# Other orders for the written work lists of a one-core convolution and attention kernel

## The chip, the cores and the metric

The kernel runs on one core of a Trainium2 chip. The metric is the device time of one execution in microseconds (us). The engines are TensorE (PE, matrix products), VectorE (DVE), ScalarE (ACT), GpSimd (POOL) and SyncE (SP, which issues most of the transfers between the chip's memory and the core's buffers). Each engine works through its own instructions in order; semaphores hold it back where it needs another engine's or a transfer's result.

## The reference

The input is 8 images of 512 channels by 32 x 32 points, all in 32-bit floats. Each image goes through two layers with a residual connection:

```python
# layer 0
x = x + L0(_gn(x))          # _gn: 32 groups of 16 channels
#   t = silu(bn(conv1x1(x)))              512 -> 512 channels, halves y0, y1
#   twice: z = silu(bn(conv3x3(y)))       256 -> 256
#          q, k, v = conv1x1(z)           4 heads of 64
#          a = softmax(q (k + rw + rh)^T / 8)
#          y_next = y + silu(bn(conv1x1(a v)))
#   silu(bn(conv1x1(concat(y0, y1, y2, y3))))     1024 -> 512
# layer 1
x = x + L1(_gn(x))
#   h = prune(relu(bn(depthwise3x3(x))), 4.0)
#   prune(relu(bn(conv1x1(h))), 0.001)            512 -> 512
```

`prune` sets a whole channel to zero when its largest magnitude lies under the limit. Attention runs over all 1024 points of an image, in each of the two inner blocks.

## The kernel before

The images come one after another (b = 0 to 7). A channel block of 128 partitions by 1024 points is the usual tile. The program does not write its instructions in a fixed sequence of loops. Each stage adds small closures, called pieces here, to named queues (`add`, line 306), and `go` (line 309) takes them from the queues in the order of a written list of names: `Q*3` is three pieces of queue Q. There are four lists: FIRST (lines 45 to 60) is all of image 0 up to the middle of its layer 1, HEAD the start of images 1 to 7 (with what remains of the image before), TAIL the rest of images 1 to 6, and LAST the rest of image 7. For image 7 HEAD leaves out the words that prepare a following image (`PREPARATION`).

`InOrder` (line 93) ties every instruction of PE, DVE, ACT and SP to the one issued before it on its engine, so that these four engines execute in exactly the order of the lists. Its line 103 makes all those calls; almost every row of the profile has line 103, and the rows must be told apart by their tiles. POOL is not tied.

The names that matter, with the function that defines them:

- `conv3` (line 737), the 3x3 convolution in a transformed form: `d` makes the input's combinations on DVE, `P` the products on PE (16 products of 128 x 128 x 128 and one 1 MB weight tile for each piece), `Rc` (ACT) and `R`, `B`, `E` (DVE) transform back, `Ez` (ACT) is the activation into z. `X` and `S` load ACT's tables for exp and silu.
- `qkv` (line 903): `k`, `v`, `q` on PE; `ka`, `va`, `qa` copy the results out. `kp` (image 0) adds the position terms on POOL; `kd` (later images) adds them by a transfer from POOL's queue that accumulates into kr, read from r in the chip's memory.
- `positions` (line 894): `rk` builds a tile `pos` on DVE and stores it to r, four times in all, in image 0.
- `attention` (line 984), 32 steps for each inner block: `s` scores on PE, `e` exponential on ACT into a work buffer, `p` adds up e on DVE, `w` values on PE, `h` (ACT) and `z` (DVE) join the two accumulators; `n` sums over partitions on PE, `nr` reciprocal on DVE, `ns` spreads it over all partitions by 8 transfers (rw<-r) on SP, `nc` checks (ACT), and `sc` multiplies z by rw on DVE, four pieces.
- `cv2m` (line 1096): `m` (PE), `ma` (ACT), `mr` (DVE), the block's closing 1x1 convolution and residual.
- The large 1x1 convolutions use a seven-product scheme over quarters of the weights: layer 0's first (`ct`, `c ck cu ca`, `y yk yu ya`), its last (`quartered`, line 1262: `r0` to `r3`, `Q`, `K`, `u0 u1`, `a0 a1`, `x0 x1`) and layer 1's (`ot`, `o ok ou oa`, `O Ok Ou Oa`). Image 0 uses plain weights (`last_conv`, line 1123: `Q K u A x`), image 7 for its last two.
- `combine_weights` and `combine_more` (lines 1192 and 1223), queue `cw`, in image 0 only: 12 pieces that load weights into ht (ht<-in_w), add and subtract quarters into tiles `scomb` and store quarters and sums to the chip's memory (q<-ht, q<-scomb, s<-ht, s<-scomb).
- `layer1_front` (line 578): statistics `i im id iv ip ib`, normalised copy `b`, centre tap `bm`, eight taps `t` for each channel block on DVE, `l` relu, `lr` and `lp` the prune test. `layer1_back` (line 623): products `o`, ends `oa`, prune test `fr`, and `f`, the residual and the store of the output.
- `dp` loads the next image to pt (4 x 512 KB), `dx` loads the same image to xt again for the residual, `dw` loads wm2, `g gm gd gv gp gb ga` normalise pt; `rg` (line 1376) is the range check of the softmax sums: `least` and then `decide`, a matmul pk on PE and the flag on DVE.

Large weights pass through a ring of 5 buffers of 8 KB for each partition (`ring_load`, line 412): when a tile's product is issued, the load of the tile five places on follows on SP. Temporary tiles (e, sum, rw, pos, scomb, mid, ...) share one pool, `work`, of 11 buffers of 4 KB for each partition; a new tile waits until all that read or wrote its buffer before, transfers included, is done. So the order of the lists also decides which tiles share a buffer, and which engine waits for which transfer.

Of the kernel before, what the change touches and what calls it, by code (L numbers as in the profile page):

```python
# [15 lines left out]
P = 128  # L16
B, C, F = 8, 512, 32
# [27 lines left out]
FIRST = """  # L45
    g*6 gm gd gv g gp g gb gm gd ga gv ga c gp fo gb c ta0 ga ta0 ga ta0 ti0 fo ta2 to0*2 c ti0*2
    ca ta2*2 c rl ca ta1*3 ti2 ti1 to1 d ti1 d y ya to1 ti1 y ya ti2 to2 d ti2 d to2 rl d*2 y ya
    y ya P*2 Rc R Rc d dw d*3 R d*2 P Rc P*3 Rc R B*2 R B Rc R E Ez B Rc R E Ez ta0 k*3 ka kp k X
    ka q*4 ta0*2 qa*2 v ti0 to0 ta1*2 to0 s e ti0*2 kp ta1 v va v*2 va ti1 s ti1*2 w s*2 e*2 w s
    e*2 p*3 w s*2 p ta2 e w*2 to1 e s*2 w p*2 s e p e w to1 e w ta2 s h p z e ta2 s e w*2 p s*2  # L50
    ti2 e*2 p w to2*2 s e s w*2 e p w*2 ti2*2 s*2 e*2 w p*2 s*2 w h e w s e w s e p s w s e*2 p*5
    n nr p z rh ns e p nc sc s e w*2 s*2 w*2 e*2 s w s*2 w h s z w sc e*4 w p*4 s w*2 e w p*2 w
    nc p n dp h z S nr nc*2 ns sc*2 Q m ma K mr m ma m*2 ma*2 mr*2 Q K mr d*7 P*2 Rc R d P Rc R
    Rc d*2 R d P Rc d R B*2 P Rc R E B P Rc Ez R B E Ez k cw rk X k*3 ka kp ka kp cw*3 v*2 va v*2
    va q rk q qa q cw s e cw q qa s e p w s*2 e p e p w cw s*2 dx w e p s e p e s e p*2 w*3 s e w
    g s e w h z s*2 e w s e w s g*2 s w p s*2 e*2 cw e cw w*2 e s p*2 w*2 s*2 cw w p*2 e p e*3 rk
    p cw*2 h p s z e s e w s e w rk p g p w*2 p w s n p nr s*2 e ns p*2 sc e w e nc s*2 g*3 e w s
    e*2 s e p w h s e nc w s e g p*3 w*3 p*2 w*3 sc w p h z*2 Q S n nr nc ns sc Q gm m ma mr sc
    m*3 ma*2 mr*2 ma mr Q u Q A x gd u Q A x gv i gp nc i*3 Q im id Q iv ip ib b gb A x bm i ga*4
    t i t*3 ct Q ct Q A x i*2  # L60
"""

HEAD = """
    c*4 ck cu ct*2 ca cu t im c cu*2 c*2 id iv cu y ca t cu*2 ca yk ca y*2 ip y t*2 d yu d ya y
    ib yu d*2 P d yu d*2 b P Rc R b bm d P d*2 y Rc R Rc b d R d B P Rc l B lr R B P Rc R E B P
    Rc R E Ez*2 yu bm*2 y lp yu ya yu*2 k t*19 v*2 va k*2 ya*2 ka k ka v*2 va X l kd q*2 qa lr lp
    t kd q s e t q qa s e p w s e s e p w*2 s*2 e*2 w s*2 w*2 s e*2 w s w e*2 s p*5 h e l w s*2 w
    e*2 lr t s w*2 p*2 e s e s e t w s w*2 z e s*2 e w e s w s*2 h e p e w s*2 p*5 z w e*3 s*2 e
    t w e p*2 s*2 e*2 w*2 l lr w p ot s p*2 e p*3 lp w h z n nr nc ns p*2 w lp w s*2 w e s w*2
    e*2 w*3 p sc p sc nc S p ot h z n nr o ok o ns O Ok ou oa ot*2 O sc m sc ma m ma Ou Oa m mr  # L70
    ma m ma O o mr*3 Ou ou d o d ou o O*2 d*2 P Ou ou Ou d*2 o ou d Rc ou nc R oa d*2 Ou oa P Rc
    d nc O P R d*2 P Rc P R B Oa Rc P R Ou Oa B*2 Rc B Rc R E R E Ez*2 o O k*4 ou oa Ou Oa ka*2
    fr*3 v*2 va q*2 v*2 dp qa g va g q X kd f g f kd s e q qa fr f*2 dx s e w s*2 e w e s*2 w s*2
    e*4 p*2 w s g*3 p*3 g s w*2 e s w*2 e*2 s*2 w g h s w e*2 w p*4 s*2 w s*2 w p*2 s*2 e p w e*6
    p w*2 h s*2 e*2 z p*4 w p*2 s e s z e w p*2 s n nr ns e w*4 nc s nc s e w p e w h s*2 w sc w
    e w s*2 e*3 w s p e p sc p*4 w*4 z n h z nr S ns
"""

TAIL = """
    r2 r0 Q*3 r0 sc*2 r0*2 m*2 r1 m ma gm m nc gd ma gv r1 ma r3 mr*2 K mr r2 r3 gp r2 ma mr r1  # L80
    gb ga r1 K ga ct r2 Q r3 Q*4 u1 u0 r3 Q u0*4 Q u0 Q a1 Q a0 x0 a0 ga x0 i a0 x0 i*3 im u0 a0
    id x1 ga ct Q iv ip Q u1 x0 ib b i u1 i bm t u1 t Q*2 u1 t*2 u1*2 a1 x1 a1*2 x1*2 i*2 nc
"""

LAST = """
    Q*2 nc sc m sc nc rg m*3 ma*3 mr ma mr*3 Q A Q x i*2 im id Q iv ip Q ib Q A x b bm i*2 t*2 im
    id Q iv t*2 ip t*2 ib t b bm t*2 Q A x i*2 t Q l lr lp t im id t Q A iv ip t Q ib b bm t*4 x
    t A x t i*2 l lr o*2 t im id o iv t lp ip t ib o*2 rg b bm t*4 l lr t lp t*5 l lr lp o*20 oa
    o oa o*6 fr f oa*2 fr f oa*2 fr f oa*2 fr f
"""  # L90


# [1801 lines left out]
```

## Time and profile before

| what | value |
|---|---|
| median of 4 runs | 2582.24 us (2581.66 to 2582.9) |
| profiled run, its own time | 2583.75 us |
| its span, first to last instruction | 2581.8 us |
| granted TensorE clock, mean | 0.995 |
| busy: PE, DVE, ACT, POOL | 2535.8, 2074.2, 1205.5, 126.4 us |
| bytes moved by DMA | 284.38 MB, mean 110 GB/s |
| output stores (out<-xt) | 32 of 512 KB, 7.2 us to land (median) |
| image loads xt<-in_x, pt<-in_x | 32 of 512 KB each, 6.9 and 11.6 us |
| ring loads wring<-u | 96 of 1 MB, 4.8 us |
| row spreads rw<-r | 256 of 64 KB, 2.0 us |

The profile is of one execution. A row of a timeline has its start (us from the start of the span), its length, the engine, the line, the operation, output<-input, how many instructions were merged, and in brackets the idle time of the engine before it with what ended it. A row of waits has who waited for whom, the total, how often, and the longest. A row of windows has the stretch, its length, then for PE, PEld (weight load), DVE, ACT and POOL the busy time and the count, then PE's granted clock (1.00 is full), the busy share of the DMA engines, and GB/s. Each fp32 matmul is two records. The profiled run is compared with itself; times of runs are compared with the median.

### The profile page before, as it was taken

The numbers are of one execution on the slowest core, as the hardware profiler recorded it, in microseconds if no ns is written. First come the engines' busy times: TensorE is split into PE (matmuls) and PEld (weight loads), VectorE is DVE, ScalarE is ACT, GpSimd is POOL, SyncE is SP. The second block draws the span as 40 slices with busy tenths as digits, with TensorE's granted clock in tenths as the row PEclk, the third lists the DMA queues.
The fourth block names the chain that finished last, engine by engine and source line by source line (L and its number), as shares of the span: only waits on it lengthen the run. The fifth ranks groups of instructions, "written<-read, shape, count | busy, mean of one in ns | idle before, by whom it ended". The sixth has DMA issues, their size and how long they took to land.

```text
span 2581.8 us, 38500 instructions
## 1 busy us (share of the span) xinstructions
PE 2535.8 (98%) x15518; PEld 1329.9 (52%) x15518; DVE 2074.2 (80%) x2992; ACT 1205.5 (47%) x1595; POOL 126.4 (5%) x100
## 2 busy tenths in 40 slices
PE   7998999999999999999999999999999999999997
PEld 4463464644646346463464634646455554656443
DVE  7877599866988779886798868988699876998647
ACT  3634347353472634635355353644436454373524
POOL 1000000000000000000000000000000000000000
PEclk9999999999999999999999999999999999999998
DMA  9357141341414324052240612407133160422400
GB/s 347 120 174 254 60 153 36 105 164 59 148 33 149 115 71 141 32 183 80 74 145 17 225 39 82 137 19 245 32 110 94 50 214 31 140 65 86 123 17 34
DMA packets 116393, 284.38 MB, mean 110 GB/s; under 512 B 10608, under 2 KB 76400, under 8 KB 101872
## 3 DMA queue, kind: packets, MB, share of 16 engines
q1 hardware_dynamic: 108624, 263.76, 29.5%
q0 software_dynamic: 4032, 14.68, 3.1%
q10 hardware_dynamic: 3552, 3.41, 0.4%
q8 instruction: 124, 2.03, 0.3%
q14 instruction: 61, 0.50, 0.1%
HBM read 226.24 MB, written 38.80 MB: 103 GB/s over the span
## 4 chain that ended last, share of the span: by engine, by line
PE 72%; DVE 20%; DMA 3%; ACT 2%; issue 2%; SPq 1%; ACTq 0%; POOL 0%; DVEq 0%
PE ps_s L103 15%; PE ps_av L103 14%; PE ps_qk L103 8%; PE ps_q L103 7%; PE ps_c L103 6%; PE ps_cv L103 6%; PE ps_cv2q L103 6%; PE ps_m L103 4%; PE ps_v L103 4%; DVE ht L103 3%; DVE mid L103 3%; DVE sum L103 2%; SPq L103 1%; DVE y L103 1%; DVE vtmp L103 1%
## 5 line engine op out<-in xcount | busy, mean ns | idle before, releaser
L103 ACT ACTIVATE e<-ps_s 128x1024 f32<-128x1024 f32 x512 | 504.2, 1022 | 237.1 <-PE ps_s L103 185.5
L103 PE MATMUL ps_s<-qy,kr 64*64 64x512 f32 x4096 | 518.6, 592 | 6.1 <-ACT e L103 6.0
L103 PE MATMUL ps_av<-e,vt 64*64 64x512 f32 x4096 | 518.8, 593 | 0.0
L103 DVE TENSOR_TENSOR sum<-sum,e 128x1024 f32<-128x1024 f32 x384 | 468.5, 1220 | 58.0 <-ACT e L103 30.7
L103 DVE SCALAR_TENSOR_TENSOR ht<-xn,v_sb,ht 128x961 f32<-128x961 f32 (+1 forms) x256 | 319.3, 1252 | 8.3 <-ACT ht L103 3.1
L103 PEld LDWEIGHTS ps_s<-qy,kr 64*64 64x64 f32 x4096 | 172.5, 132 | 278.0 <-issue 133.0
L103 PEld LDWEIGHTS ps_av<-e,vt 64*64 64x64 f32 x4096 | 185.1, 133 | 253.5 <-issue 226.8
L103 PE MATMUL ps_qk<-z,wring 128*128 128x512 f32 x512 | 232.8, 598 | 2.3 <-ACT z L103 1.9
L103 PE MATMUL ps_q<-pt,wring 128*128 128x512 f32 x392 | 176.8, 594 | 0.0
L103 DVE TENSOR_TENSOR sum<-e 128x1024 f32<-128x1024 f32 x64 | 78.1, 1221 | 106.3 <-ACT e L103 66.8
L103 ACT COPY c<-ps_c 128x256 f32<-128x256 f32 x96 | 35.8, 373 | 262.8 <-PE ps_c L103 259.6
L103 PEld LDWEIGHTS ps_qk<-z,wring 128*128 128x128 f32 x512 | 94.6, 190 | 120.0 <-issue 99.6
L103 PEld LDWEIGHTS ps_c<-vt,wring 128*128 128x128 f32 x1024 | 118.7, 194 | 11.7 <-issue 6.7
L103 PE MATMUL ps_c<-vt,wring 128*128 128x128 f32 x1024 | 119.6, 277 | 4.8 <-DMA wring<-u 4.8
L103 PEld LDWEIGHTS ps_c<-kr,wring 128*128 128x128 f32 x1024 | 117.9, 192 | 11.4 <-issue 8.3
L103 PE MATMUL ps_v<-wring,z 128*128 128x256 f32 x512 | 117.9, 381 | 0.9 <-DVE kr L103 0.3
L103 PE MATMUL ps_c<-kr,wring 128*128 128x128 f32 x1024 | 118.1, 275 | 0.1
L103 PE MATMUL ps_c<-qy,wring 128*128 128x128 f32 x1024 | 117.0, 275 | 0.0
L103 PEld LDWEIGHTS ps_c<-qy,wring 128*128 128x128 f32 x1024 | 115.6, 192 | 0.0
L103 PE MATMUL ps_m<-z,wm_sb 128*128 128x512 f32 x256 | 113.9, 594 | 0.0
L103 PEld LDWEIGHTS ps_q<-pt,wring 128*128 128x128 f32 x392 | 71.7, 190 | 81.0 <-issue 72.5
L103 ACT ACTIVATE m<-ps_m,bi,sc 128x512 f32<-128x512 f32 x64 | 49.8, 778 | 134.9 <-PE ps_m L103 133.8
(189 smaller groups left out, 3298.6 us busy)
## 6 DMA issues: line engine op xcount, KB each, us to landing
wring<-u SPq DMA_DIRECT2D x96, 1024.0 KB, 4.8
wring<-q SPq DMA_DIRECT2D x28, 896.0 KB, 4.8
pt<-in_x SPq DMA_DIRECT2D x32, 512.0 KB, 11.6
rw<-r SPq DMA_DIRECT2D x256, 64.0 KB, 2.0
xt<-in_x SPq DMA_DIRECT2D x32, 512.0 KB, 6.9
out<-xt SPq DMA_DIRECT2D x32, 512.0 KB, 7.2
kr<-r POOLq DMA_DIRECT2D x28, 512.0 KB, 6.0
wring<-in_wqkv SPq DMA_DIRECT2D x16, 768.0 KB, 4.3
```

The costliest lines, as they stand in the source:

```text
L103: made = method(*args, **kwargs)
```

## The change

Only the four strings are changed. Each list holds the same pieces as before, and each queue keeps its own order; what differs is the order among queues, and with it the order of instructions on PE, DVE, ACT and SP, the sharing of work buffers, and the waits. The first 70 pieces of FIRST are the same. In FIRST the stores of weight sums (`cw`) and positions (`rk`), `dx`, `dw` and ACT's `S` stand elsewhere; in HEAD `dp`, `dx`, `f`, the taps `t` and `sc`; TAIL starts with `sc` instead of `r2 r0 Q`; in LAST the second `rg` and the closing `o oa fr f`.

```diff
@@ -45,48 +45,49 @@
 FIRST = """
     g*6 gm gd gv g gp g gb gm gd ga gv ga c gp fo gb c ta0 ga ta0 ga ta0 ti0 fo ta2 to0*2 c ti0*2
     ca ta2*2 c rl ca ta1*3 ti2 ti1 to1 d ti1 d y ya to1 ti1 y ya ti2 to2 d ti2 d to2 rl d*2 y ya
-    y ya P*2 Rc R Rc d dw d*3 R d*2 P Rc P*3 Rc R B*2 R B Rc R E Ez B Rc R E Ez ta0 k*3 ka kp k X
-    ka q*4 ta0*2 qa*2 v ti0 to0 ta1*2 to0 s e ti0*2 kp ta1 v va v*2 va ti1 s ti1*2 w s*2 e*2 w s
-    e*2 p*3 w s*2 p ta2 e w*2 to1 e s*2 w p*2 s e p e w to1 e w ta2 s h p z e ta2 s e w*2 p s*2
-    ti2 e*2 p w to2*2 s e s w*2 e p w*2 ti2*2 s*2 e*2 w p*2 s*2 w h e w s e w s e p s w s e*2 p*5
-    n nr p z rh ns e p nc sc s e w*2 s*2 w*2 e*2 s w s*2 w h s z w sc e*4 w p*4 s w*2 e w p*2 w
-    nc p n dp h z S nr nc*2 ns sc*2 Q m ma K mr m ma m*2 ma*2 mr*2 Q K mr d*7 P*2 Rc R d P Rc R
-    Rc d*2 R d P Rc d R B*2 P Rc R E B P Rc Ez R B E Ez k cw rk X k*3 ka kp ka kp cw*3 v*2 va v*2
-    va q rk q qa q cw s e cw q qa s e p w s*2 e p e p w cw s*2 dx w e p s e p e s e p*2 w*3 s e w
-    g s e w h z s*2 e w s e w s g*2 s w p s*2 e*2 cw e cw w*2 e s p*2 w*2 s*2 cw w p*2 e p e*3 rk
-    p cw*2 h p s z e s e w s e w rk p g p w*2 p w s n p nr s*2 e ns p*2 sc e w e nc s*2 g*3 e w s
-    e*2 s e p w h s e nc w s e g p*3 w*3 p*2 w*3 sc w p h z*2 Q S n nr nc ns sc Q gm m ma mr sc
-    m*3 ma*2 mr*2 ma mr Q u Q A x gd u Q A x gv i gp nc i*3 Q im id Q iv ip ib b gb A x bm i ga*4
-    t i t*3 ct Q ct Q A x i*2
+    y ya d P Rc R P d*3 Rc R d*2 P Rc R B P Rc R B*3 P*2 Rc R E Ez Rc R E Ez k*3 ka k ka kp X ta0
+    q*2 qa ta0*2 ti0*2 kp v s e v va v*2 va ta1 ti0 ta1*2 to0*2 q*2 qa ti1 dw s w e p s e s e w s
+    ti1 s ti1 to1 e*2 p w p*3 w s e w ta2 w s e w to1 s e p*2 s e w h z p s e p ta2*2 s w*2 e s w
+    s e s e ti2*2 w*2 p to2 s w p*2 ti2 e to2 s e w e s e w h p*2 s e s w s*2 e w e s*2 p*4 w*2 n
+    e nr e p z s p e p e s rh nc w e w s ns sc w*2 e s*2 w h s w*2 s e*4 w z sc w p s w*2 e w h p
+    nc p*5 n nr z ns sc*2 dp nc*2 Q m*2 ma*2 m*2 K ma mr Q ma mr*3 d*4 S K P*2 d*3 Rc R d Rc R P
+    Rc d*2 R d cw d B*2 P Rc R P Rc R E Ez B P B k Rc R E Ez cw k*2 ka X dx g k ka kp cw*3 kp rk
+    q*2 qa rk v*2 va v*2 va q s e q qa s e p cw*2 w s e p s e w*2 s*2 e w s*2 e*3 p*5 w s*2 e w e
+    p w*2 h z s e s w*3 cw s*2 e*2 w p cw w cw p*2 s g s e*3 w s*2 w e p*2 s e*2 p g s e w h s e
+    rk s p z w e s e w s cw*2 p e p w*2 g rk p*2 s n nr e s e p*2 w s*2 p g e ns g w*3 p nc s e h
+    s w e*2 s*2 e*2 p sc nc S p*2 w*3 g*2 p w*4 sc p z h z Q n nr Q gm nc ns sc m ma m ma sc mr m
+    ma nc gd gv gp m mr ma mr*2 Q*3 gb Q u A u x i*2 A x i*2 im id Q A iv ip x ib b bm t ga t
+    ga*3 i*2 t Q*2 ct*2 A t x i*2
 """
 
 HEAD = """
-    c*4 ck cu ct*2 ca cu t im c cu*2 c*2 id iv cu y ca t cu*2 ca yk ca y*2 ip y t*2 d yu d ya y
-    ib yu d*2 P d yu d*2 b P Rc R b bm d P d*2 y Rc R Rc b d R d B P Rc l B lr R B P Rc R E B P
-    Rc R E Ez*2 yu bm*2 y lp yu ya yu*2 k t*19 v*2 va k*2 ya*2 ka k ka v*2 va X l kd q*2 qa lr lp
-    t kd q s e t q qa s e p w s e s e p w*2 s*2 e*2 w s*2 w*2 s e*2 w s w e*2 s p*5 h e l w s*2 w
-    e*2 lr t s w*2 p*2 e s e s e t w s w*2 z e s*2 e w e s w s*2 h e p e w s*2 p*5 z w e*3 s*2 e
-    t w e p*2 s*2 e*2 w*2 l lr w p ot s p*2 e p*3 lp w h z n nr nc ns p*2 w lp w s*2 w e s w*2
-    e*2 w*3 p sc p sc nc S p ot h z n nr o ok o ns O Ok ou oa ot*2 O sc m sc ma m ma Ou Oa m mr
-    ma m ma O o mr*3 Ou ou d o d ou o O*2 d*2 P Ou ou Ou d*2 o ou d Rc ou nc R oa d*2 Ou oa P Rc
-    d nc O P R d*2 P Rc P R B Oa Rc P R Ou Oa B*2 Rc B Rc R E R E Ez*2 o O k*4 ou oa Ou Oa ka*2
-    fr*3 v*2 va q*2 v*2 dp qa g va g q X kd f g f kd s e q qa fr f*2 dx s e w s*2 e w e s*2 w s*2
-    e*4 p*2 w s g*3 p*3 g s w*2 e s w*2 e*2 s*2 w g h s w e*2 w p*4 s*2 w s*2 w p*2 s*2 e p w e*6
-    p w*2 h s*2 e*2 z p*4 w p*2 s e s z e w p*2 s n nr ns e w*4 nc s nc s e w p e w h s*2 w sc w
-    e w s*2 e*3 w s p e p sc p*4 w*4 z n h z nr S ns
+    ct c*4 ck cu*2 ct ca c cu im c*2 t id y cu*2 ca iv t cu y*2 t ca cu t ca yk y ip l d y yu d
+    ib ya b d*3 yu d yu P Rc d P R Rc d*2 R P d Rc R d*2 P Rc R B*2 b*2 P*2 Rc R B lr E Rc R B bm
+    y E Ez*2 y lp yu bm yu ya t yu t yu t*2 bm k v*2 t*8 ya va k ka k*2 t*3 ka v*2 t va l lr q*2
+    qa ya t*3 X q kd*2 s e lp q qa s e w s e s e w*2 s e s e w s p*3 s p e*2 p*3 t*2 w s*2 e w*3
+    s*2 w e t l h s e*2 w s*2 p w p ot e*3 s*2 e p*2 z w p s p*2 e*2 s p e p t lr w*4 s*2 w h s*2
+    z lp e w s*2 e*5 w p w s t p e w*2 s*2 e*2 p*3 n nr p l w*2 h p z nc s p w e ns lr lp s e w*3
+    s*2 w e nc e w*3 h p*4 ot n nr nc z ns nc ot o*2 ok ou S oa sc*2 ot O Ok O sc m sc ma m ma O
+    m*2 o*2 Ou Oa mr Ou ma mr*2 ma mr d ou O d*2 o d*2 ou P Rc d*2 Ou R ou d o P d*2 O Ou Rc ou
+    oa ou oa Ou Oa P Rc O P dp R*2 d Rc d P R P Rc B*2 R E B Ez Rc R o O B E Ez Ou k Ou ou q Oa q
+    qa oa k v ka v*3 va*2 k*2 ka q Oa g fr*2 X kd s e q qa kd f*2 fr g*2 s w e p s*2 e p w s*2 e
+    p e*2 w s*2 w s p*2 e*2 p*2 s fr w s*2 w*2 f w g e*4 f h s*2 e w e p*3 s w e g s e p w s*2 w
+    s e*3 s e w g*2 w p*2 g w p z w h s e s p w e w s e p*2 s p*3 e p w s dx e s e n nr nc z p ns
+    sc w*2 s e p w s e p w*2 h s w s*2 e p w*3 s w z sc e*2 p*2 e w*2 p w h z S n nr ns nc
 """
 
 TAIL = """
-    r2 r0 Q*3 r0 sc*2 r0*2 m*2 r1 m ma gm m nc gd ma gv r1 ma r3 mr*2 K mr r2 r3 gp r2 ma mr r1
-    gb ga r1 K ga ct r2 Q r3 Q*4 u1 u0 r3 Q u0*4 Q u0 Q a1 Q a0 x0 a0 ga x0 i a0 x0 i*3 im u0 a0
-    id x1 ga ct Q iv ip Q u1 x0 ib b i u1 i bm t u1 t Q*2 u1 t*2 u1*2 a1 x1 a1*2 x1*2 i*2 nc
+    sc*2 nc r2 r0 r2 r0 Q*3 gm gd r0 m ma m mr gv m r1 r3 Q r0 m Q ma mr ma mr r2 r1 gp gb ma mr
+    r1*2 r3 r2 r3 ga*2 K*2 Q u0 Q ct a0 Q u0 Q u1 r3 Q u0*3 a0 a1 x0 u0 i*2 x0 a0 x0 i Q x1 Q i*2
+    u0 i a0 im Q x0 id iv ip ga*2 ct ib b bm nc u1 Q u1*2 t u1 t Q*2 t u1 a1 t u1 x1 a1 x1 a1 x1
+    i*2
 """
 
 LAST = """
-    Q*2 nc sc m sc nc rg m*3 ma*3 mr ma mr*3 Q A Q x i*2 im id Q iv ip Q ib Q A x b bm i*2 t*2 im
-    id Q iv t*2 ip t*2 ib t b bm t*2 Q A x i*2 t Q l lr lp t im id t Q A iv ip t Q ib b bm t*4 x
-    t A x t i*2 l lr o*2 t im id o iv t lp ip t ib o*2 rg b bm t*4 l lr t lp t*5 l lr lp o*20 oa
-    o oa o*6 fr f oa*2 fr f oa*2 fr f oa*2 fr f
+    Q*2 sc nc*2 rg sc m ma m*2 ma mr*2 m ma*2 mr*2 Q A x i*2 Q*2 im Q A id iv ip Q ib b x i*2 bm
+    t im t Q id iv t*2 ip t ib b bm t*4 Q A x i*2 t l lr Q lp t im id Q A t*2 iv ip t ib b t*2 bm
+    t x t Q A x t o i*2 o*2 t im id l lr t o*2 iv ip t ib lp b bm t*2 l t lr rg t*2 lp t*5 l lr
+    lp o*22 oa*2 fr f oa o*3 oa fr f o*2 oa*2 fr f oa*2 fr f
 """
 
 
```

## Prediction

> **What bounds the kernel now.** I read the page's busy times and chain first.
>
> ```profile
> PE 2535.8 (98%) x15518; PEld 1329.9 (52%) x15518; DVE 2074.2 (80%) x2992; ACT 1205.5 (47%) x1595; POOL 126.4 (5%) x100
> ...
> PE 72%; DVE 20%; DMA 3%; ACT 2%; issue 2%; SPq 1%; ACTq 0%; POOL 0%; DVEq 0%
> ```
>
> PE is busy for 98% of the span, and the change leaves it the same 15518 matmuls. So nothing can be won but the time in which PE stands still or runs at half clock; that "busy" holds half-clock time too. The waits of PE, longest first, say where it stands, and their windows say in which list:
>
> ```profile
> PE pm L103 <- DVE mv L103: 13.6, 5, 8.1
> PE ps_s L103 <- ACT e L103: 6.0, 4, 3.4
> PE ps_c L103 <- DMA wring<-u: 4.8, 1, 4.8
> PE ps_dn L103 <- DVE sum L103: 3.8, 6, 0.9
> ```
>
> The first (8.1 us) and third (4.8 us, at 58 us) lie in the start of FIRST, whose first 70 pieces stay; the third waits for a load that those pieces issue. The second is the place to look at: PE, ACT and SP's queue around 250 us, each from its timeline, and PE's granted clock in between.
>
> ```profile
> 248.75 1.33 PE L103 MATMUL ps_s<-qy,kr 64*64 64x512 f32 x8 [2.11 <-ACT e L103]
> ...
> 258.39 1.09 PE L103 MATMUL ps_s<-qy,kr 64*64 64x512 f32 x8 [3.42 <-ACT e L103]
> ```
> ```profile
> 247.67 1.94 ACT L103 ACTIVATE e<-ps_s 128x1024 f32<-128x1024 f32 x2 [4.98 <-DMA s<-scomb]
> ...
> 257.31 1.02 ACT L103 ACTIVATE e<-ps_s 128x1024 f32<-128x1024 f32 x1 [4.89 <-DMA r<-pos]
> ```
> ```profile
> 235.16 2.51 SPq L103 DMA_DIRECT2D xt<-in_x  x4
> 237.71 2.82 SPq L103 DMA_DIRECT2D s<-scomb  x4
> 241.34 0.55 SPq L103 DMA_DIRECT2D ht<-in_w  x1
> 251.22 1.53 SPq L103 DMA_DIRECT2D s<-ht  x3
> 252.87 0.63 SPq L103 DMA_DIRECT2D r<-pos  x1
> ```
> ```profile
> 244.00:249.80 5.80, 3.69 (x36) 1.02 (x32) 4.71 (x4) 1.94 (x2) 0.00 (x0) 0.97 1.01 356
> 249.80:252.90 3.10, 3.10 (x20) 1.07 (x16) 1.57 (x3) 1.61 (x2) 0.00 (x0) 0.50 0.32 91
> 252.90:259.70 6.80, 3.38 (x32) 0.97 (x28) 6.76 (x9) 1.50 (x2) 0.00 (x0) 1.00 1.03 357
> 259.70:263.10 3.40, 3.40 (x20) 1.05 (x16) 3.19 (x3) 1.47 (x2) 0.00 (x0) 0.50 0.18 72
> ```
>
> An exponential e twice waits for a work buffer that a store still reads. SP's queue is in order: the image load xt (4 x 512 KB) sits just ahead of the stores of scomb; the next weight load (ht) takes until 251.2 while the DMA engines are full (share 1.01, 356 GB/s), and the store of pos, queued behind stores that need that load, leaves only at 252.87. Each stall is followed by some 3.4 us at clock 0.50. The timeline of PE has 104 score and value matmuls from 243.46 to 264.18 us; 4 of them back to back take 0.43 us, so they need 11.2 of 20.7 us: 9.4 us are lost here (0.1 off for the last one's end).
>
> **The change part by part.** The sum is made against the profiled run, 2583.75 us (span 2581.8, 1.95 around it), which lies 1.5 us above the median of the four runs.
>
> *FIRST, weight sums, positions and dx.* dx now comes in layer 1's key stage, some 21 us of PE work ahead of the last weight load, and so out of the full stretch. From each store's piece to the piece that takes its buffer next, counted in listed PE pieces (0.86 us a score or value piece, 1.72 a key, value or query projection), the cover was 6.9 us twice for scomb and 0.9 us for the last pos. In the new lists it is 9.5, 8.6, 4.3, 1.7, 3.5 and 5.2 us, and only one of the three short ones is taken by an e: 4.3 and 1.7 us are a scomb and a pos on DVE, which has slack (64.54 us busy in 200 to 285 us). A store needs its issue (0.6 us) and 2.4 us to land at least, 5.2 in the median, 9.1 at most. So DVE waits 1.5 and 2 us, of which I count half to reach PE, and e (3.5 us cover) 1 to 2 us: 3 us stay, 9.4 - 3 = 6.4 us gained. Bounds: all of it gained, or a loss of 3 us (a store landing after 9.1 us, three times, each 4 us over its cover).
>
> *Clock.* An idle time of 1.60 us (layer 1's first key product, 195.1 us) left the clock at full, one of 2.11 us halved it for 3.4 us (1.7 us lost). My 3 us are pieces under 2 us, so no half clock is added; one wait of 3 us would add 1.7. [...]
>
> *FIRST, elsewhere.* Close Ez of the second half now stands ahead of Rc on ACT at layer 1's keys (1.60 us idle on ACT z): 0.7 us won, but a weight sum (2 x 0.6 us) comes in on DVE there: nothing. dw (one load) moves past ring loads whose tiles are used five tiles later: nothing; without that cover 4.8 us, wring's landing.
>
> *HEAD, seven times.* The image period is 313.0 us, 308 of it PE's pieces at their back-to-back pace; most of the rest are switches that stay. What goes is in the waits of ps_dn: the softmax sums' second n waits for the last p on DVE, because sc0 and sc1 stand before it and wait for eight row spreads by DMA:
>
> ```profile
> 770.18 0.69 DVE L103 TENSOR_TENSOR z<-z,rw 128x512 f32<-128x512 f32 x1 [1.34 <-DMA rw<-r]
> ...
> 772.75 0.69 DVE L103 TENSOR_TENSOR z<-z,rw 128x512 f32<-128x512 f32 x1 [0.74 <-DMA rw<-r]
> ```
>
> In the new layer 0, sc0 and sc1 follow the last p, n and ns. DVE gets 2.1 us of waits and 1.3 us of work off the way to n; n1 begins 0.45 to 1.45 us (mean 0.97) behind the pieces' pace, 0.2 of it the switch. Gain 0.75 an image. What is late next: sc2, behind the second n's spreads, reaches the first m some 0.35 us late by the rows' durations. Net 0.4, bounds +1 and -1 (the longest n1 wait, either sign). The taps t no longer come 19 in a row after the first k: DVE is full there (40.45 of 40.80 and 29.43 of 30 us), but its work up to layer 0's last E is the same within 0.1 us (43.6 against 43.5 us), so the wait of 0.34 us at v stays. dp (pt load) moves ahead of the last two P of layer 1, past their ring loads and the accumulating kd loads of POOL; ring tiles have five tiles of cover, kd some 3 us: nothing, without cover 2 to 6 us (kd lands in 6.0). Output stores and dx come later, dx still some 20 us ahead of x: nothing. 7 x 0.4 = 2.8 us gained (-7 to +7).
>
> *TAIL.* sc comes first, so DVE waits about 5 us (eight spreads at 0.6 us of issue, 2.0 to land) without r's before it. The first product that needs all r0 has 17 us of PE pieces before it (Q, Q, half Q, three m, half Q, m), DVE's work to there 5 us of wait and 9 us of instructions: nothing; 3 us of cover. If it is gone, some 2 us an image.
>
> *LAST.* Its end is DVE's taps: flag waited for PE (1.25 us), on the way to the last tap.
>
> ```profile
> 2546.70 0.15 DVE L103 TENSOR_SCALAR flag<-pk 1x1 int32<-1x1 f32 x1 [1.25 <-PE pk L103]
> ...
> 2565.12 1.13 PE L103 MATMUL ps_pw<-ht,wring 128*128 128x512 f32 x2 [0.87 <-ACT pw L103]
> ```
>
> rg's second half now stands after the third lr, where PE comes to its matmul pk straight from the last statistics (iv), with no o pieces before it, and has it done long before DVE asks: 1.2 us gained. In the second row a product waited for an oa that reads the other half of its PSUM tile; in the new list no product stands behind an oa of its own tile: 0.8. Output stores keep their order: together 2 us (0 to 3).
>
> Sum: 2583.75 - 6.4 - 2.8 - 2.0 = 2572.5, less 1.5 to the median: **2571 us**.
>
> **The rivals.**
> - *The stall in FIRST stays in another place* (the 1.7 and 3.5 us covers): for it, DMA was full there and the sums keep their bytes; against it, the bytes of xt are gone from that stretch. Gain 2.8 + 2.0 only: 2577.4.
> - *Slower: layer 1's first P waits in every image.* In HEAD before, six pieces of 1.72 us lie between the last m and the first P of layer 1 (10.3 us); in the new list four (6.9 us). On the way stand ma (0.78), the last mr (0.6), four d (two at 1.2, the last two together 2.4) and ou (0.6): 6.8 us, so the cover is about nothing, and what delays DVE there, as sc2's wait, goes to PE. Against it: DVE is 51.26 of 60 us busy from 720 to 780, so it should come to m on time. It decides from (6.4 + 2.8 + 2.0)/7 = 1.6 us an image; at 3 us, 2571 + 21 = 2592 (one image's DVE wait for rw, longest 4.1, makes this the likely top).
> - *No difference:* PE's work is equal, and gains of FIRST are given back by half a microsecond to 1.5 an image: 2577 to 2587.
>
> **How the numbers follow.** The forecast 0.45 (2562 to 2575), FIRST's stall stays 0.17 (2575 to 2579), slower by P 0.28 (2587.5 to 2600), no difference 0.10. The measurement can tell about 0.2%, 5.2 us: faster is below 2577, slower above 2587.4. Half of the rival at 2577.4 is same. Faster 0.45 + 0.09 + 0.01 = 0.55, same 0.16, slower 0.29. The range leaves out 0.05 below 2558 (all of FIRST, +7 in HEAD) and 0.12 above 2595.
>
> **What would show it.** In the changed kernel's trace: no e row with a wait of over 2.5 us for DMA s or r, and clock 1.00 from 240 to 270 us (FIRST); the row ps_dn waiting for sum under 1 us in all and an image period of 312.6 us (HEAD); no row of PE waiting for kr at layer 1's first P (rival); flag without its 1.25 us (LAST). I am wrong if the image period grows: seven times any small wait outweighs the one stall.

## The result

The changed kernel takes 2579.35 us (median of 32 runs, 2575.61 to 2583.71); the kernel before, run beside it, 2582.69 us (median of 52 runs). The ratio is 0.9986, with a 95% interval of 0.9981 to 0.9991: 3.6 us (2.3 to 4.9) less, under the 0.2% that counts as a change here. 11 us had been forecast. The profiled run has a span of 2578.4 us, 3.4 less than before.

The busy times and the chain on the changed kernel's page, to be held against the two lines shown of the kernel before:

```profile
PE 2530.1 (98%) x15518; PEld 1309.9 (51%) x15518; DVE 2074.5 (80%) x2992; ACT 1206.9 (47%) x1595; POOL 143.5 (6%) x100
...
PE 91%; DVE 6%; DMA 1%; ACT 1%; SPq 1%; issue 0%; POOL 0%; ACTq 0%; DVEq 0%; POOLq 0%
```

The chain now runs through PE for 91% instead of 72%. That alone tells little: it says that DVE stands less often on the path, and not that PE loses less time. What PE waits for tells more:

```profile
PE pm L104 <- DVE mv L104: 12.2, 4, 8.0
PE ps_cv L104 <- DVE c L104: 5.1, 6, 0.9
PE ps_av L104 <- ACT e L104: 4.2, 1, 4.2
PE pv L104 <- DVE d L104: 3.9, 4, 1.4
PE ps_c L104 <- DMA wring<-u: 3.9, 1, 3.9
PE ps_pw L104 <- DVE wring L104: 2.2, 1, 2.2
PE ps_qk L104 <- ACT z L104: 2.0, 1, 2.0
...
PE ps_dn L104 <- DVE sum L104: 0.3, 1, 0.3
```

The waits of ps_s for e (four, 6.0 us) and of ps_dn for sum (3.8 us, now 0.3) have gone or shrunk, as forecast. Others are new or longer: ps_cv for c, six times 0.85 us, once in each TAIL; pv for d, two more than before, in TAIL of images 2 and 6; ps_av for e, 4.2 us in FIRST; ps_pw for wring in LAST. The wait of ps_qk for z stands elsewhere: 2.0 us at layer 0's keys in FIRST, instead of 1.6 at layer 1's.

Where the time went, list by list. A list's time runs from the start of its first product to that of the next list's; the records of PE were put to the pieces of the lists in order.

| stretch | before, us | changed, us | difference | forecast |
|---|---|---|---|---|
| up to the first product | 8.14 | 7.99 | -0.2 | 0 |
| FIRST | 327.95 | 323.53 | -4.4 | -6.4 |
| HEAD, seven | 1798.6 | 1788.9 | -9.7 | -2.8 |
| TAIL, six | 335.6 | 344.5 | +8.9 | 0 |
| LAST to its last product | 101.1 | 102.3 | +1.2 | -2.0 |
| last product to the end of the span | 10.4 | 11.2 | +0.8 | |
| sum | 2581.8 | 2578.4 | -3.4 | -11.2 |

HEAD wins more than three times what was forecast and TAIL gives nearly all of it back. Every sign that the forecast had named came true: no e of layer 1's attention in FIRST waits for a store, the clock is 1.00 from 240 to 270 us, ps_dn waits 0.3 us in all, no first P of layer 1 waits in images 1 to 7, flag waits no more, and the image period is 312.6 us in four images of six. That period was met by luck, because HEAD's extra gain and TAIL's loss cancel; with images 2 and 6 the mean is 313.0 us, against 312.9 before. The signs looked only where the forecast expected something.

**TAIL.** PE and DVE in TAIL of image 2 of the changed kernel, from their timelines:

```profile
912.97 0.39 PE L104 MATMUL pv<-d,g_sb 128*128 128x4 f32 x2 [0.72 <-DVE d L104]
...
921.88 1.88 PE L104 MATMUL ps_cv<-qy,wring 128*128 128x512 f32 x4
924.61 0.70 PE L104 MATMUL ps_cv<-qy,wring 128*128 128x512 f32 x1 [0.85 <-DVE c L104]
```
```profile
905.13 0.69 DVE L104 TENSOR_TENSOR z<-z,rw 128x512 f32<-128x512 f32 x1 [4.09 <-DMA rw<-r]
909.16 0.69 DVE L104 TENSOR_TENSOR z<-z,rw 128x512 f32<-128x512 f32 x1 [3.33 <-DMA rw<-r]
...
923.87 0.69 DVE L104 TENSOR_TENSOR c<-part,ps_cv 128x512 f32<-128x512 f32 x1 [0.30 <-PE ps_cv L104]
```

The new list has `Q u0 Q`: the first Q completes a12 of one half of the output channels, u0 reads it on DVE, and the second Q writes a12 of the other half. Both halves lie in one PSUM tile (the `big_tile` of line 1306 before the change), so the second Q waits until u0 has read: 2.73 us from the start of one Q to that of the next instead of 1.72. That makes a TAIL of 57.05 us instead of 55.93. DVE's waits for row spreads, at the start of TAIL, are 5.9 to 6.4 us in four images and stay covered there. In images 2 and 6 the second one comes later (3.33 us in the rows above, 3.57 in image 6, 1.8 to 2.3 in the others), and TAIL takes another 1.0 and 1.2 us. The product that then waits is pv, the word `gv`, whose input d comes from DVE behind the two sc (first row).

**FIRST.** ACT, PE and PE's clock at the end of layer 1's attention:

```profile
275.94 1.02 ACT L104 ACTIVATE e<-ps_s 128x1024 f32<-128x1024 f32 x1 [8.00 <-DVE z L104]
```
```profile
267.53 5.33 PE L104 MATMUL ps_av<-e,vt 64*64 64x512 f32 x48
277.02 1.98 PE L104 MATMUL ps_av<-e,vt 64*64 64x512 f32 x8 [4.16 <-ACT e L104]
```
```profile
265.00:271.60 6.60, 6.60 (x68) 2.40 (x64) 6.36 (x9) 2.31 (x3) 0.00 (x0) 1.00 0.20 59
271.60:275.00 3.40, 1.26 (x12) 0.15 (x4) 3.37 (x5) 0.00 (x0) 0.00 (x0) 1.00 0.00 0
...
277.00:280.50 3.50, 3.48 (x11) 1.12 (x12) 2.52 (x3) 2.33 (x5) 0.00 (x0) 0.55 0.00 0
```

No e waits for a store any more. But the last e takes the buffer of rw, and the last to read rw is the second sc, which DVE reaches at 275.2 us: DVE is full there (6.36 of 6.60 us, 3.37 of 3.40). The half clock follows as before (0.55 in the last row). FIRST also lost where the forecast had not looked, at layer 0's first key product:

```profile
72.33 3.75 PE L104 MATMUL ps_qk<-z,wring 128*128 128x512 f32 x8 [1.97 <-ACT z L104]
```

which in the kernel before was

```profile
71.57 4.83 PE L103 MATMUL ps_qk<-z,wring 128*128 128x512 f32 x10 [0.34 <-ACT z L103]
```

**LAST.** PE, then the window rows:

```profile
2535.17 0.38 PE L104 MATMUL pm<-mv,g_sb 128*128 128x1 f32 x2 [1.95 <-DVE mv L104]
...
2541.10 26.15 PE L104 MATMUL ps_pw<-ht,wring 128*128 128x512 f32 x54 [2.22 <-DVE wring L104]
```
```profile
2538.70:2541.00 2.30, 0.18 (x2) 0.08 (x2) 1.82 (x5) 0.59 (x1) 1.39 (x1) 0.50 0.00 0
2541.00:2544.40 3.40, 3.30 (x4) 1.51 (x5) 3.36 (x3) 2.79 (x3) 0.00 (x0) 0.50 0.00 0
```

Twenty-seven products of 0.86 us stand behind the second prune (wring), and the first of them run at half clock. PE, not the taps, sets the end. What follows the last product takes 0.8 us longer; why was not tried apart.

### The profile page after: what moved, and what is told of

Its sections match the earlier page's. It is cut to its first block, busy times and chain, and to the rows that moved or that the text cites. A ratio compares the mean times of both kernels' runs of the same rounds, so it can differ in the third digit from the quotient of the medians.

```text
span 2578.4 us, 38524 instructions
## 1 busy us (share of the span) xinstructions
PE 2530.1 (98%) x15518; PEld 1309.9 (51%) x15518; DVE 2074.5 (80%) x2992; ACT 1206.9 (47%) x1595; POOL 143.5 (6%) x100
## 3 DMA queue, kind: packets, MB, share of 16 engines
q10 hardware_dynamic: 3552, 3.41, 0.4%
## 4 chain that ended last, share of the span: by engine, by line
PE 91%; DVE 6%; DMA 1%; ACT 1%; SPq 1%; issue 0%; POOL 0%; ACTq 0%; DVEq 0%; POOLq 0%
PE ps_s L104 17%; PE ps_av L104 16%; PE ps_q L104 13%; PE ps_c L104 12%; PE ps_qk L104 8%; PE ps_cv2q L104 8%; PE ps_cv L104 6%; PE ps_v L104 4%; PE ps_m L104 4%; PE ps_dn L104 1%; PE ps_pw L104 1%; DVE sum L104 1%; DVE ht L104 1%; SPq L104 1%; DVE mid L104 0%; DVE kr L104 0%
## 5 line engine op out<-in xcount | busy, mean ns | idle before, releaser
L104 DVE TENSOR_TENSOR sum<-sum,e 128x1024 f32<-128x1024 f32 x384 | 483.9, 1260 | 42.8 <-ACT e L104 14.8
L104 PE MATMUL ps_av<-e,vt 64*64 64x512 f32 x4096 | 499.4, 591 | 4.2 <-ACT e L104 4.2
L104 PE MATMUL ps_s<-qy,kr 64*64 64x512 f32 x4096 | 500.9, 591 | 0.0
L104 DVE SCALAR_TENSOR_TENSOR ht<-xn,v_sb,ht 128x961 f32<-128x961 f32 (+1 forms) x256 | 314.0, 1232 | 9.4 <-ACT ht L104 4.7
L104 PEld LDWEIGHTS ps_av<-e,vt 64*64 64x64 f32 x4096 | 175.9, 133 | 263.3 <-issue 233.3
L104 PEld LDWEIGHTS ps_s<-qy,kr 64*64 64x64 f32 x4096 | 159.8, 132 | 282.0 <-issue 154.7
L104 PEld LDWEIGHTS ps_c<-kr,wring 128*128 128x128 f32 x1024 | 117.9, 192 | 11.4 <-issue 8.8
L104 DVE TENSOR_TENSOR z<-z,rw 128x512 f32<-128x512 f32 x64 | 43.5, 688 | 84.7 <-DMA rw<-r 83.9
```

Source lines behind the costliest of these rows:

```text
L104: made = method(*args, **kwargs)
```

## The experiments

Ratios are to the kernel before, run beside each, with 95% intervals. Each kernel had its profile taken once.

**One list at a time.** Each kernel has one of the four new strings and the other three as before:

```diff
-FIRST = """ (as before) """     HEAD, TAIL, LAST as before
+FIRST = """ (as in the change) """
```

> FIRST alone in the new order. Theory (each list acts by itself): FIRST takes 4.4 us less, as between the two traces (327.95 to 323.53 us from its first to its last product), and the total falls by 4.4 us (0.17%). Rival (the lists act on each other through buffers and late engines): the total moves by less than 2 us, because what FIRST wins the old HEAD loses at its start.

Measured: 2580.53 us, 0.9993 (0.9984 to 1.0002), 1.8 us less and not clear of nothing. FIRST took 324.87 us. Beside it stands what one profile could not tell: FIRST in its old order varies from run to run. In seven profiles it took 324.88 to 327.95 us, 326.4 in the mean; the one that the forecast was read from was the longest. Much of the spread comes near its start: PE's wait at about 50 us, put down to a weight load in five of the seven, took 2.6 to 4.8 us. In the new order, four profiles, it took 323.01 to 326.85, mean 324.6. Its share is 1.8 us, by both ways. Neither theory had that number; the old HEAD lost nothing to it (257.05 us an image).

> HEAD alone in the new order. Theory: each of seven HEADs takes 1.4 us less (256.9 to 255.5 us), the total falls by 9 to 10 us (0.37%). Rival: HEAD's gain is bought with late row spreads that the old TAIL then waits for, so that TAIL grows and the total falls by less than 4 us.

Measured: 2571.61 us, 0.9962 (0.9949 to 0.9976); each HEAD 255.5 us, TAIL 55.93 as before. The theory holds; the rival's growth of TAIL did not come.

> TAIL alone in the new order. Theory: a product that writes one half of a shared PSUM tile waits for the sum u0 that reads the other half, about 1.0 us in each of six images, so each TAIL takes 57.0 instead of 55.9 us and the total rises by 6 to 7 us (0.25%). Rival: TAIL's loss comes from sc standing first behind the late row spreads of the new HEAD; with the old HEAD the total rises by less than 2 us.

Measured: 2589.07 us, 1.0032 (1.0020 to 1.0044); each TAIL 57.05 us. PE's waits in images 1 to 6 of this run:

```profile
PE ps_cv L104 <- DVE c L104: 5.1, 6, 0.9
PE ps_dn L104 <- DVE sum L104: 3.7, 5, 1.2
```

The same six waits stand there with the old HEAD, so they belong to TAIL's own order; the second row is HEAD's old wait. The extra 1.0 and 1.2 us of images 2 and 6 are not there. Late second spreads that cost PE time came in five of the six profiles that have the new HEAD together with the new TAIL (or TAIL with the one exchange below), in one or two images each, and in none of the profiles with only one of the two. What delays them was not tried.

> LAST alone in the new order. Theory (products o wait for the second prune, which stands 2.7 us later, and then run at half clock): the total rises by 1.9 us (0.07%). Rival (the forecast's step: flag off the tap chain): the total falls by 1 to 2 us.

Measured: 2583.06 us, 1.0005 (0.9996 to 1.0014): unclear in time. PE waited 2.28 us for wring as in the changed kernel; LAST took 100.8 us to its last product, less than in the changed kernel: the 54 records behind that wait took 25.11 us instead of 26.15, the four behind pm 1.96 instead of 2.81, so less of it ran at half clock by these rows. From there to the end it took 10.95 us. A fall of more than 1.0 us is outside the interval, which leaves only the edge of the forecast's 1 to 2; the theory's rise of 1.9 us is inside.

The four ratios together come to 2 us less, and the whole change to 3.6. Within the noise of that sum, some 6 us, this is what lists give that act independently.

**The shared PSUM tile.** All four new lists, with one exchange in TAIL:

```diff
-ga*2 K*2 Q u0 Q ct a0 Q
+ga*2 K*2 Q*2 u0 ct a0 Q
```

> All four new lists, but in TAIL both second halves of the a12 products come before the first u0. Theory (shared PSUM tile): TAIL falls from 57.0 to about 56.0 us, the total by 6 us against the changed kernel, to 0.9963 of the kernel before. Rival (sc first, DVE late by its 7.4 us of waits for row spreads): the wait only moves to a later product, the total falls by less than 2 us.

Measured: 2574.24 us, 0.9964 (0.9951 to 0.9978); TAIL 55.93 us in every image, 2 and 6 included. PE in TAIL of image 2:

```profile
919.48 3.60 PE L104 MATMUL ps_cv2q<-kr,wring 128*128 128x512 f32 x8
922.91 3.60 PE L104 MATMUL ps_cv<-qy,wring 128*128 128x512 f32 x8
926.35 3.60 PE L104 MATMUL ps_cv2q<-z,wring 128*128 128x512 f32 x8
```

No gap is left, and nothing in PE waits between images 1 and 7. The theory holds: the place of u0 between the two Q makes the 0.85 us. That the tie between them is the shared tile is read from the program; separate tiles were not tried. The run does not settle the late row spreads. They did not come in this execution (DVE's second wait is 1.8 us in images 2 and 6), and in the run with three edits below, which has the same TAIL, one came in image 6: DVE waited 3.18 us, pv 0.57, and TAIL took 56.77 us.

**The second sc in FIRST.** All four new lists, and:

```diff
-e*2 p sc nc S p*2 w*3 g*2 p w*4 sc p z h z
+e*2 p sc*2 nc S p*2 w*3 g*2 p w*4 p z h z
```

> All four new lists, but in FIRST the second sc of layer 1's first head pair follows the first one at once instead of standing 15 pieces later. Theory (the last exponential e takes the buffer of rw, and sc is the last to read rw): ACT's wait of 8.0 us shrinks to under 4, PE's 4.2 us go and the half clock behind them (1.9 us), FIRST falls by 5 to 6 us, the total to 0.9964 of the kernel before. Rival (DVE is 4 us late as a whole there, with its 0.96 busy share): the sums p come as late as before and n waits for them instead, less than 2 us gained.

Measured: 2579.72 us, 0.9991 (0.9982 to 1.0000): no gain. ACT's timeline shows why:

```profile
273.85 1.94 ACT L104 ACTIVATE e<-ps_s 128x1024 f32<-128x1024 f32 x2 [5.59 <-DVE z L104]
```

Moved earlier, sc gives up rw's buffer earlier in the list, and now an earlier e gets it; PE waited 5.2 us for that one. The wait was as the theory said (e behind sc), the cure was not. That DVE must come to sc sooner is tried next.

**DVE's backlog in FIRST.** All four new lists, with two rk (each a sum of 2.0 us on DVE and a store) taken out of the attention:

```diff
-q*2 qa rk v*2 va v*2 va q s e q qa
+q*2 qa rk v*2 va rk v*2 va q rk s e q qa
...
-p*2 s g s e*3 w s*2 w e p*2 s e*2 p g s e w h s e rk s p z w e s e w s cw*2 p e p w*2 g rk p*2 s n nr
+p*2 s g s e*3 w s*2 w e p*2 s e*2 p g s e w h s e s p z w e s e w s cw*2 p e p w*2 g p*2 s n nr
```

> All four new lists, but in FIRST the third and fourth rk (two sums of 2.0 us on DVE and their stores) stand in the value and query stage of layer 1 instead of its attention. Theory (DVE's backlog at the end of that attention is what makes e wait): DVE comes to the second sc some 4 us sooner, PE's wait of 4.2 us falls under 1 us, FIRST by 4 to 6 us. Rival (the buffer that the pool gives to e decides): PE still waits over 3 us for e.

Measured: 2573.37 us, 0.9969 (0.9958 to 0.9979). ACT's and PE's waits for e:

```profile
ACT e L102 <- DVE z L102: 5.8, 1, 5.8
```
```profile
PE ps_av L102 <- ACT e L102: 2.0, 1, 2.0
```

Between the two: the wait falls from 8.0 to 5.8 us and PE's from 4.2 to 2.0. PE's time beyond the back-to-back pace, after the 400th piece of FIRST, is 5.7 us against 7.4 to 8.7 in four profiles of the new order. So DVE's backlog carries part of the wait, and the buffer that e gets the rest. The time fell by more than these 2.6 us: 4.4 us by the two ratios, with some 3 us of uncertainty.

**The image load in FIRST.** The kernel before, with one move:

```diff
-E Ez k cw rk X k*3 ka ... p w cw s*2 dx w e p s
+E Ez k cw rk X dx k*3 ka ... p w cw s*2 w e p s
```

> The kernel before with one move: in FIRST dx, the load of xt, stands at layer 1's first key product. Theory (its 2 MB fill the DMA engines just ahead of the stores of weight sums): the exponential's two waits for DMA s and DMA r, 4.98 and 4.89 us, fall to under 2 us each and FIRST by 5 to 7 us. Rival (the buffer of a stored tile is taken again too soon, whatever the load does): both waits stay above 3 us and FIRST within 2 us.

Measured: 2577.13 us, 0.9985 (0.9976 to 0.9994), 3.9 us less; FIRST 321.0 us. ACT's waits for transfers in that stretch:

```profile
ACT e L103 <- DMA r<-pos: 3.4, 1, 3.4
```

The wait for s<-scomb is down to 0.6 us, the one for r<-pos stays at 3.4; PE waits for e once, 2.7 us, and its clock stays at 1.00 from 195 to 285 us. The load of xt was the main cause, as the forecast read it; pos's buffer is still taken too soon, as its rival had it. One move gives more than FIRST's whole new order by the ratios (3.9 against 1.8 us), though their intervals overlap. The last run below has the same FIRST; there e waited 3.9 us for r<-pos, PE 3.1 us for e, and FIRST took 323.7 us.

**The second prune in LAST.** All four new lists, and:

```diff
-im id l lr t o*2 iv ip t ib lp b bm t*2 l t lr rg
+im id l lr t lp o*2 iv ip t ib b bm t*2 l t lr rg
```

> All four new lists, but in LAST the second lp stands before the o pieces and the statistics iv, as it did in the kernel before. Theory (PE's last 27 products wait 2.2 us for the scaled weights and lose some more to half clock): LAST falls by 2 us, the total to 0.9978 of the kernel before. Rival (the last prune on DVE sets the end, as in the kernel before): less than 0.5 us.

Measured: 2577.89 us, 0.9983 (0.9974 to 0.9992), against 0.9986 of the changed kernel: not told apart by time. LAST itself took 99.1 us to its last product, where five profiles with the new LAST had 100.8 to 102.3. PE:

```profile
2537.37 4.56 PE L104 MATMUL ps_pw<-ht,wring 128*128 128x512 f32 x10
2542.74 12.28 PE L104 MATMUL ps_pw<-ht,wring 128*128 128x512 f32 x28 [0.82 <-DVE flag L104]
2555.41 7.11 PE L104 MATMUL ps_pw<-ht,wring 128*128 128x512 f32 x16 [0.39 <-DVE wring L104]
```

The wait of 2.22 us is gone, and the products reach the last prune (wring, 2555.41) with 0.39 us to wait: here DVE's taps set the end again. In the traces the theory holds, without the half clock in this part of LAST (1.00 from 2531 to 2560 us).

**The three edits together** (TAIL, sc, lp):

> All four new lists with the three edits together. Theory (three separate places): the gains add, 12 to 14 us below the changed kernel, about 2566 us, 0.9936 of the kernel before. Rival (each time the next late engine shows up): less than 8 us below the changed kernel.

Measured: 2570.01 us, 0.9957 (0.9944 to 0.9971). By the ratios that is 7.5 us below the changed kernel, by the medians 9.3: the sum of the TAIL and lp edits (5.7 and 0.8 us by their ratios) within the noise, at the edge of the rival's 8 and short of the theory's 12 to 14. The theory had counted 5 us for the sc edit, which is worth nothing.

**The flag in LAST.** The kernel before, with one move:

```diff
-ib o*2 rg b bm t*4 l lr t lp t*5
+ib o*2 b bm t*4 l lr rg t lp t*5
```

> The kernel before with one move: in LAST the second rg stands behind the third lr. Forecast's step: flag's 1.25 us leave the chain of taps, the last prune and the end come 1.2 us sooner. Rival (PE's last products are as late as DVE's taps, so the end hangs on both): the last prune comes 1 us sooner, but the end moves by less than 0.5 us.

Measured: 2581.38 us, 0.9997 (0.9988 to 1.0006). DVE and PE:

```profile
2548.32 0.14 DVE L103 TENSOR_SCALAR flag<-pk 1x1 int32<-1x1 f32 x1
...
2559.08 0.15 DVE L103 TENSOR_SCALAR keep<-keep 128x1 f32<-128x1 f32 x1 [2.59 <-ACT over L103]
```
```profile
2543.86 17.80 PE L103 MATMUL ps_pw<-ht,wring 128*128 128x512 f32 x40
2562.53 6.28 PE L103 MATMUL ps_pw<-ht,wring 128*128 128x512 f32 x14 [0.87 <-ACT pw L103]
```

flag waits no more. Counted from the start of LAST (2468.22 us here, 2470.28 before) the last prune comes at 90.9 instead of 92.1 us, 1.2 sooner, but the product after the oa at 94.3 instead of 94.8: PE's x40 products are as long as the taps. The traces go with the rival, half a microsecond; the time tells neither 0.5 nor 1.2 us from nothing, and LAST in its old order took 100.0 to 101.6 us to its last product over seven profiles.

**HEAD, where its gain lies.** The kernel before, with sc moved:

```diff
-p sc p sc nc S p ot h z n nr o ok o ns O Ok
+p*2 nc S p ot h z n nr o ok o ns sc*2 O Ok
```

> The kernel before with one move: in HEAD the first two sc of layer 0's attention stand behind the second n instead of ahead of the last two p. Theory (the forecast's step: sc's waits for row spreads delay the last sum): n's wait goes, 0.75 us an image, HEAD about 256.1 us, the total falls by 5 us (0.998). Rival (HEAD's gain of 1.5 us lies in several places, an nc ahead of an e, the r buffer that e takes, the value product after Ez): less than 2 us gained here, 0.999 or above.

Measured: 2576.89 us, 0.9983 (0.9974 to 0.9992), 4.4 us less; HEAD 256.1 us in the mean against 256.9, and PE has no wait for sum left:

```profile
PE ps_c L103 <- DVE y L103: 0.3, 1, 0.3
```

The theory holds, with 0.9 us an image instead of 0.75. The new list has 255.5, another 0.5. The same kernel with one more move was to find it:

```diff
-lp w h z n nr nc ns p*2 w lp w s*2 w e s w*2
+lp w h z n nr ns p*2 w lp w s*2 w e nc s w*2
```

> The kernel before with sc moved as in the run that moved sc alone, and also nc, ACT's check of the first softmax sums in layer 0, one exponential later. That run left HEAD at 256.0 us against 255.5 in the new list. Theory (ACT waits for the reciprocal at nc and the next e stands behind it): the 0.40 us that a value product lost there in each image go, HEAD 255.6 us. Rival (that e is late by its scores or buffer): HEAD stays at 256.0.

Measured: 2575.94 us, 0.9973 (0.9964 to 0.9983); HEAD 255.9 to 256.7 us, no better; the total is not told apart from that of the run that moved sc alone. The value product ahead of n still takes 1.26 us instead of 0.86. The rival holds, as far as nc goes. By comparison of the two profiles the rest lies in two seams: the first v after layer 0's convolution starts 0.35 us late in the old order and not in the new one, and the value product ahead of the first n loses 0.40 in the old order and 0.18 in the new one. What makes them late was not tried apart.

**What helped, put together.** FIRST as before with dx moved, the new HEAD, the old TAIL, the new LAST with lp moved:

> What helped, put together: FIRST as before with dx early, HEAD in the new order, TAIL as before, LAST in the new order with the second lp early. Theory (places independent): FIRST 321, seven HEADs of 255.5, TAIL 55.9, LAST 99 to 100.5 us: about 2566 us, 0.9937 of the kernel before. Rival (the lists give back to each other): above 2570 us.

Measured: 2567.54 us, 0.9943 (0.9930 to 0.9957), 14.3 us under the kernel before and some 11 to 12 under the changed one. FIRST 323.7, HEAD 255.5, TAIL 55.9, LAST 99.5 us. The parts add up within a microsecond or two.

## Why the prediction was wrong, point by point

- *FIRST, weight sums, positions and dx.* The mechanism was right: the load of xt filled the DMA engines (busy share 1.01 from 244.0 to 249.8 us) ahead of the stores, moving it frees them (dx alone: 3.9 us), and no e waits for a store in the new order. The 3 us left over were for waits that did not come: neither e nor DVE waits for a store in the new order's attention. The step "only one of the three short ones is taken by an e" counted the buffers of stored tiles alone. The buffer that cost time is rw's, taken by the last e, behind 2.0 us of pos and 2.6 us of weight sums that the change had put on DVE some 20 us before. What stayed was 4.2 us of waiting, with 3.42 us at half clock; that the 4.2 are near 3 is luck.
- *FIRST against one profile.* The 9.4 us were a true reading of one execution, but FIRST varies by 3 us. In PE's time beyond the back-to-back pace, after the 400th piece of the list, the old order has 10.1 to 12.1 us in seven profiles (mean 11.4), the new one 7.4 to 8.7 in four (mean 8.3): 3.1 us won. In the first 100 pieces the new order has 14.7 us in the mean against 13.4: 1.3 lost, mostly at layer 0's first key product (1.97 us for z). "FIRST, elsewhere ... nothing" looked only at layer 1's keys.
- *Clock.* "An idle time of 1.60 us left the clock at full, one of 2.11 us halved it" made a rule of two rows: single waits under 2 us cost no clock. A wait of 1.98 us halved it in one run (0.58 behind it), and one of 1.97 us did not in another (1.00; last section).
- *HEAD.* The wait of n was the right place, and sc the right cause: 0.9 us an image by itself, where 0.75 was forecast. Two terms were wrong: sc2's 0.35 us at the first m did not come, and "the wait of 0.34 us at v stays" did not hold: it went. 1.4 us an image instead of 0.4, outside the stated bound of 1.
- *TAIL, the step that failed.* "Nothing; 3 us of cover" put TAIL at no cost; it cost 8.9 us in the changed kernel's profile. The step is silent on `Q u0 Q`. The rule was in the forecast's own working: in LAST it counted 0.87 us for a product that waits for an oa that reads the other half of its PSUM tile. The same sight in TAIL would have given 0.85 to 1.0 us six times, 5 to 6 us; 1.12 us six times, 6.7 us, were measured. That is more than half of the error. The other 2.2 us are the late spreads of images 2 and 6. There the working took the wrong product: 17 us of PE pieces stand ahead of the one that needs all r0, but only 12 ahead of gv's pv, which needs DVE too, and DVE's 7.4 us of waits, 2.4 more than were counted, were not covered.
- *LAST.* "flag ... 1.2 us gained" holds for DVE's taps (1.2 measured), and the end gains 0.5, because PE's products are as long. Nothing was said of the second lp, which stands behind ib in the new list: the products wait 2.2 us for it and run at 0.50 behind that, to 2546.63 us. -2.0 was forecast, +1.2 to the last product came, +0.8 behind it. Part of the +1.2 is chance: the mean to the last product is 101.0 us over seven profiles of the old order and 101.7 over five of the new one.
- *The rivals.* None of them. Layer 1's first P did not wait in any image (the cover of about nothing was enough). "The stall in FIRST stays in another place" came true in half, by another buffer than the ones named. "No difference" has the right number by luck: in it too gains of one list are given back by another, but it put them into FIRST and HEAD; they were HEAD and TAIL.

Most losses were short waits of a kind that the old profile shows too, in a place where the old order has none. The forecast followed the waits that the profile named, and checked the new order only around them.

## What to carry to other kernels

When only the order changes, read the new order for every kind of wait that the old profile shows, and not only at the places where it shows them: each reader of a shared PSUM tile between two writers, each buffer that a stalled engine would have to free, each scalar that gates a long run of products. A wait of 0.85 us that recurs in each round outweighs a stall of 5 us that is there once. And take the size of a stall that hangs on transfers from several profiles: here one stretch of 328 us moved by 3 us between profiles of the same order. Name signs for the places that are expected not to change, too.

## What the runs showed of the hardware

In these traces the length of an idle time alone does not tell whether PE's clock falls behind it. The same product, in the same order of FIRST, with the same idle time ahead of it, ran at a granted clock of 1.00 in the changed kernel and of 0.58 in the run with the exchanged TAIL. PE and its clock in the changed kernel:

```profile
72.33 7.41 PE L104 MATMUL ps_qk<-z,wring 128*128 128x512 f32 x16 [1.97 <-ACT z L104]
```
```profile
72.30:75.00 2.70, 2.67 (x6) 1.16 (x7) 2.11 (x5) 0.49 (x2) 0.00 (x0) 1.00 0.00 0
```

and in the run with the exchanged TAIL:

```profile
72.42 8.83 PE L104 MATMUL ps_qk<-z,wring 128*128 128x512 f32 x16 [1.98 <-ACT z L104]
```
```profile
72.40:75.00 2.60, 2.58 (x4) 1.18 (x5) 2.11 (x5) 0.39 (x2) 0.00 (x0) 0.58 0.00 0
```

1.97 and 1.98 us of idle time, 7.41 and 8.83 us for the same 16 records: 1.4 us apart. What decided it is not shown.

The same holds within one profile. PE's idle times of 1.5 us or more, from 60 us to the last product, and the stretch at 0.50 that began during the wait or within 1.4 us of its end:

| kernel | wait ended at, us | idle time, us | clock 0.50 from, us | for, us |
|---|---|---|---|---|
| before | 195.10 | 1.60, for z | none | |
| before | 248.75 | 2.11, for e | 249.47 | 3.41 |
| before | 258.39 | 3.42, for e | 259.71 | 3.41 |
| before | 2540.20 | 2.64, for mv | 2539.81 | 6.83 |
| changed | 72.33 | 1.97, for z | none | |
| changed | 277.02 | 4.16, for e | 276.76 | 3.42 |
| changed | 2535.17 | 1.95, for mv | 2536.39 | 10.24 |
| changed | 2541.10 | 2.22, for wring | at 0.50 already | |

In the changed kernel 1.95 us of waiting had a fall behind it and 1.97 us had none. LAST's spread shows it too: behind the wait for mv, 1.95 us in both, the four records of ps_pw took 2.81 us in the changed kernel and 1.96 in the run of the new LAST alone, and the 54 behind wring, after 2.22 and 2.28 us, 26.15 and 25.11. In its new order LAST took 100.8, 100.8, 102.0, 102.3 and 102.3 us to its last product in five profiles, with 2.2 to 2.3 us of waiting for wring in each.
